# Matrices by turns with the normalisation, filter tables in three buffer sets asked for two steps ahead, and the first set loaded in pieces beside attention

## The chip, the cores and the metric

The kernel runs on one core of a Trainium2 chip. The core has five engines with instruction streams of their own: TensorE (PE in the profile; its weight loads are listed apart as PEld), VectorE (DVE), ScalarE (ACT), GpSimd (POOL) and SyncE (SP, which here only issues DMAs). The metric is the device time of one execution in microseconds.

## The reference

The input is an image tensor of 2 batches, 128 channels and 64 x 64 pixels, so 4096 tokens of 128 channels per batch. Layer 0 normalises over groups of channels and applies rotary attention with four heads, a projection and a residual. Layer 1 does this on the tokens:

```python
t = t + _L1_attn_ref(_ln_t(t))       # softmax(x x^T) x, one head of 128
t = t + _L1_ffn_ref(_ln_t(t), ...)   # STU
```

The second line is a spectral filter. Sixteen filters `phi` (4096 long) are convolved causally with every channel, once as they are and once with alternating signs; the 16 x 2 results of 128 channels are mixed by matrices `M_phi_plus` and `M_phi_minus` scaled by `sigma ** 0.25`, and a short autoregressive term over three taps (`M_u`) is added. Four branches of this kind are weighted by a straight-through choice of `softmax(log_weights + gumbel)`; the branches differ in the length of the sequence that they see, and in their matrices.

## The kernel before

**Layer 0** (`layer0`) goes through four units (batch, pair of heads). In each, two heads times eight blocks of 512 queries are worked through in eleven groups of up to three key tiles: scores on PE (tile `s`), an exponential on ACT (`e`), the weighted sum on PE (`acc`, in PSUM), and at the end of a block a copy to `accs` on DVE (L413). `divide` normalises that with a reciprocal that goes through DRAM by SyncE (`rec`, `back`, `accs<-back`), `project` adds it to the tokens.

Other work is laid beside these groups by Python generators: at certain group numbers `next(beside)` lets one step of it be written into the program. In the last unit the numbers are `BESIDE_LAST`, five of eleven, so 80 slots, and the work is `beside_last`: statistics of batch 0 (nine steps), `normalise` (17; it makes `hi`, `lo`, `bothT`, which are the two halves of the normalised tokens in f16, straight and transposed), `filters16` (12; it makes the filters' spectra and writes them with 32 DMAs and two copies to the DRAM tensor `tables16`) and `matrices16` (33). The last one loads for each of 16 filters the four branches' matrices (`room<-in_mpp`, `room<-in_mpm`, two buffers), takes their weighted sum on DVE (`weighted_sum`, L750 and L752) and writes it to DRAM (`mx`). What is left of the steps is written after the loop.

**Attention of layer 1** (`attend16`) runs for batch 0 and then batch 1 over 36 blocks (j, i) with i not below j. For each block: 24 score matmuls (`y`), exponentials on ACT, a split into two f16 parts (`pair`: a cast on ACT, L1198, a subtraction on DVE, L1199), a transposition of both parts by SyncE's DMA (`eT<-pair`, L1204, only where i is above j), and 12 matmuls of weighted sums with the straight part (`od`) and 12 with the transposed one (`oa`), two blocks later. Beside batch 0 goes the rest of layer 0 (`left`), the statistics of batch 1, `rest16` (masks and means: `mask`, `mu`, `gw`) and the normalisation of batch 1. Beside batch 1 goes `feed(0)`, which transforms the tokens of batch 0, writes them to DRAM (`rows<-uh`) and writes the autoregressive term there too (`base<-oc`), on POOL's queue for batch 0 and SyncE's for batch 1. There are four slots for a block.

**The filters** (the last part, from about 1680 us) run 64 steps (batch, half `ro`, chunk `ch` of eight, stream `s`). A step loads two 1 MB halves of tables and two tiles of tokens (`chunk16`, L1486 and L1491), convolves (16 matmuls `cv`, evacuated by ACT and DVE into two f16 parts `x`) and mixes (48 matmuls `m`). The mixing of one step is written in four parts between the four convolution parts of the next. Tables and tokens have two buffer sets, by turns: the first in a pool of its own (`tables_a`, `early`), the second in the space of `hi` and `lo` (`tables_b`). The loads of a step are written just ahead of its convolution. Beside the first 16 steps goes `feed(1)`, then `back` (L1652 to L1700), which loads `had<-base`, transforms back and adds.

**Order.** A planner with costs of its own orders each engine's instructions and sets the waits; what is written first has priority, and an instruction that is ready can be placed ahead of earlier ones. `tc.keep_in_program_order(ins)` pins an instruction behind the one written just before it on the same engine. The matmuls of `product` and of the filters' steps, and the normalising instructions (`normed`, L743) are pinned. The loads of tables and tokens are not.

Of the kernel before, what the change touches and what calls it, by code (L numbers as in the profile page):

```python
# [32 lines left out]
BESIDE_LAST = (1, 3, 5, 6, 9)  # L33
# [43 lines left out]
def conv_attn_hybrid(ctx: ExitStack, tc: tile.TileContext, io):  # L77
# [39 lines left out]
    def chain(*parts):  # L117
        for p in parts:
            yield from p
# [638 lines left out]
    def layers(st, layer0, in_halves):  # L758
# [52 lines left out]
        def filters16(spare):  # L811
# [21 lines left out]
            yield  # L833
# [115 lines left out]
        def beside_last(stage, spare=None):  # L949
# [4 lines left out]
            yield from normalise(0, stats, lambda i, n: stages[n][:, i])  # L954
            if in_halves:
                yield from filters16(spare)
                yield from matrices16(spare)
# [70 lines left out]
        def means(p, wbr):  # L1028
# [3 lines left out]
            aside.dma_start(gw, io["gw16" if in_halves else "gw"])  # L1032
            if in_halves:
                nc.vector.scalar_tensor_tensor(
                    gw, gw, OUT_SCALE, mask.unsqueeze(1).to_broadcast([P, 2, P]), ALU.mult, ALU.mult
                )
            else:
                nc.vector.tensor_tensor(gw, gw, mask.unsqueeze(1).to_broadcast([P, 2, P]), ALU.mult)

        def rest16(p):  # L1040
            wbr, top = chosen[:2]
            mask_of(p, top)
            yield
            means(p, wbr)
            yield
# [13 lines left out]
        def attend(b, p, beside, closed, ready=lambda i: None):  # L1059
# [111 lines left out]
            for _ in beside:  # L1171
                pass

# [123 lines left out]
        def feed(b, p, bank, fw, stats=None):  # L1297
# [13 lines left out]
            def taps(i, uT):  # L1311
                oc = p.tile([P, 4, P], F32, tag="oc", name=f"oc{b}_{i}", bufs=1)
# [77 lines left out]
        with ExitStack() as l1:  # L1390
# [3 lines left out]
            with ExitStack() as part:  # L1394
# [28 lines left out]
                own = (rest16(p),) if in_halves else (filters(p, fw), matrices(p))  # L1423
                steps = chain(left, stats.steps(), *own, normalise(1, stats, stage, gate))
                (attend16(0, p1, steps, closed) if in_halves else attend(0, p1, steps, closed, ready))
            right0.close()
            if in_halves:
                early = pool(middle, "early", side="right")
                tables_early = [early.tile([P, BP, NS, 2 * NK], F16, name=f"tables_a{n}") for n in range(2)]
                tokens_in = [  # L1430
                    [early.tile([P, NS, C], F16, name=f"tokens{turn}_{n}") for n in range(2)] for turn in range(2)
                ]
            if in_halves:
# [3 lines left out]
            with ExitStack() as part:  # L1437
# [12 lines left out]
                (attend16 if in_halves else attend)(1, p1, feed(0, p, bank, fw), closed)  # L1450
# [7 lines left out]
        if in_halves:  # L1458
            tables_in = [
                tables_early,  # L1460
                [px.tile([P, BP, NS, 2 * NK], F16, tag=f"b{n}", name=f"tables_b{n}") for n in range(2)],
            ]
# [5 lines left out]
        def ordered(instruction):  # L1468
            return tc.keep_in_program_order(instruction)

        def one_bank(name):
            return pc.tile([P, 512], F32, tag="bk", name=name)

# [397 lines left out]
```

## Time and profile before

| | us |
|---|---|
| median of three runs | 2745.54 |
| lowest and highest | 2739.54, 2754.03 |
| the profiled execution | 2742.39 |
| its span, first to last instruction | 2740.6 |
| PE busy | 2579.5 (94%) |
| ACT busy | 1839.1 (67%) |
| DVE busy | 1671.6 (61%) |
| POOL busy | 434.1 (16%) |
| mean granted TensorE clock | 0.98 |

By the trace, layer 0 ends at about 1047 us, the first attention at about 1350, the second at 1680, and the filters take the rest. The profile's matmuls are pipelined and their ends are modelled, so PE's busy time is an upper bound of its work. An arrow in a row means that the left side was waited for, or made, from the right side: `tables_b<-tables` is the load of the tile `tables_b` from the DRAM tensor `tables16`. A wait is put down to what came last. Idle time of an engine that bounds nothing costs nothing. The DMA share is the mean busy share of the 16 DMA engines.

### The profile page before, as it was taken

What the parts mean: (1) busy time and instruction counts of PE and PEld (TensorE: products, weight loads), DVE (VectorE), ACT (ScalarE), POOL (GpSimd) and SP (SyncE); (2) the same over time, 40 slices, a digit from 0 to 9 for tenths busy, and PEclk for the clock granted to TensorE, in tenths of its full rate; (3) what the DMA queues carried; (4) which work ended last, traced back from release to release, by engine and by line L of the source; (5) the groups of instructions that cost most, each with busy time, mean ns of one, the idle gap of its engine ahead of it and who ended that gap; (6) DMA issues with size and microseconds to landing.
All of it is one profiled execution on the core that took longest, in us unless ns stands there. A gap on an engine that the chain in (4) does not pass through costs nothing.

```text
span 2740.6 us, 32562 instructions
## 1 busy us (share of the span) xinstructions
PE 2579.5 (94%) x11955; PEld 1275.5 (47%) x11955; DVE 1671.6 (61%) x2946; ACT 1839.1 (67%) x2059; POOL 434.1 (16%) x711
## 2 busy tenths in 40 slices
PE   5999999999998897899999997999889999999998
PEld 3555555555544453344444443444344445445444
DVE  5256464246358225787887677666556666666664
ACT  4999999999998895566655564444335554555553
POOL 2022021012122301100053101111111111111110
PEclk9999999999999998999999998999999999999999
DMA  5122120012103505676475665666656656656662
GB/s 146 35 66 66 60 74 20 5 53 66 30 29 93 82 7 91 129 123 108 77 151 119 133 108 105 151 177 169 156 156 187 186 192 183 202 195 180 154 197 91
DMA packets 351051, 311.92 MB, mean 114 GB/s; under 512 B 292816, under 2 KB 303200, under 8 KB 334432
## 3 DMA queue, kind: packets, MB, share of 16 engines
q1 hardware_dynamic: 295376, 231.71, 33.3%
q0 software_dynamic: 52512, 74.81, 11.7%
q10 hardware_dynamic: 2992, 3.22, 0.4%
q8 instruction: 96, 1.57, 0.2%
q14 instruction: 75, 0.61, 0.1%
HBM read 212.53 MB, written 23.33 MB: 86 GB/s over the span
## 4 chain that ended last, share of the span: by engine, by line
PE 66%; DMA 14%; DVE 10%; ACT 7%; issue 2%; SPq 0%; POOL 0%; ACTq 0%; DVEq 0%; POOLq 0%
PE m L1565 18%; PE acc L209 12%; PE s L209 11%; PE cv L1549 6%; ACT e L465 5%; PE od L1213 5%; PE y L1185 4%; PE oa L1213 4%; DMA tables_b<-tables 4%; DMA tables_a<-tables 2%; DMA eT<-pair 2%; DMA had<-base 2%; DMA rows<-uh 2%; DVE pair L1199 1%; DVE x L1557 1%
## 5 line engine op out<-in xcount | busy, mean ns | idle before, releaser
L465 ACT ACTIVATE e<-s 128x1536 f16<-128x1536 f32 (+1 forms) x704 | 938.7, 1425 | 54.8 <-PE s L209 50.2
L1557 DVE TENSOR_TENSOR x<-cv,x 128x1024 f16<-128x1024 f32 x512 | 602.7, 1220 | 288.7 <-ACT x L1556 288.5
L1556 ACT CAST x<-cv 128x1024 f16<-128x1024 f32 x512 | 493.8, 1016 | 405.2 <-PE cv L1549 396.0
L1565 PE MATMUL m<-x,mxr 128*128 128x512 f16 x2048 | 625.1, 382 | 0.0
L209 PE MATMUL acc<-e,v 128*97 128x512 f16 x2048 | 559.5, 380 | 16.5 <-DVE accs L413 13.8
L209 PE MATMUL s<-qs,ks 128*128 128x512 f16 x2048 | 560.0, 381 | 7.9 <-ACT e L465 4.3
L1565 PE MATMUL m<-x,mxl 128*128 128x512 f16 x1024 | 393.4, 384 | 2.7 <-DVE oh L1572 2.7
L209 PEld LDWEIGHTS <-v 128*97 128x97 bf16 x2048 | 255.3, 125 | 229.9 <-issue 28.8
L1194 ACT ACTIVATE ey<-y,nshift 128x512 f32<-128x512 f32 x288 | 196.2, 687 | 196.3 <-PE y L1185 151.0
L1565 PEld LDWEIGHTS <-mxr 128*128 128x128 f16 x2048 | 201.8, 99 | 244.6 <-issue 8.2
L209 PEld LDWEIGHTS <-ks 128*128 128x128 f16 x2048 | 201.2, 99 | 230.2 <-issue 47.9
L1486 POOL DMA_DIRECT2D tokens<-rows x252 | 153.4, 613 | 841.9 <-PE cv L1549 815.4
L1185 PE MATMUL y<-bothT 128*128 128x512 f16 x864 | 204.3, 383 | 5.0 <-ACT ey L1194 4.1
L1213 PE MATMUL od<-pair,hi 128*128 128x512 f16 x576 | 185.6, 383 | 19.8 <-DVE pair L1199 14.4
L1199 DVE TENSOR_TENSOR pair<-ey,pair 128x1024 f16<-128x1024 f32 x144 | 175.2, 1219 | 37.8 <-ACT pair L1198 37.6
L1233 DVE SCALAR_TENSOR_TENSOR both<-eT 128x512 f16<-128x512 f16 x224 | 153.7, 686 | 51.6 <-DMA eT<-pair 46.7
L413 DVE COPY accs<-acc 97x512 f32<-97x512 f32 x64 | 44.2, 690 | 228.3 <-PE acc L209 228.2
L1549 PEld LDWEIGHTS <-tokens 128*128 128x128 f16 x1024 | 100.6, 99 | 158.4 <-issue 60.5
L1198 ACT CAST pair<-ey 128x1024 f16<-128x1024 f32 x144 | 150.6, 1046 | 26.6 <-DMA eT<-pair 12.6
L1213 PEld LDWEIGHTS <-hi 128*128 128x128 f16 x1024 | 101.1, 99 | 140.1 <-issue 25.6
L1565 PEld LDWEIGHTS <-mxl 128*128 128x128 f16 x1024 | 101.3, 99 | 132.4 <-DVE oh L1572 9.7
L1213 PE MATMUL oa<-eT,hi 128*128 128x512 f16 x448 | 144.2, 383 | 8.2 <-DMA eT<-pair 8.2
(221 smaller groups left out, 2294.8 us busy)
## 6 DMA issues: line engine op xcount, KB each, us to landing
tables_a<-tables SPq DMA_DIRECT2D x64, 1024.0 KB
tables_b<-tables SPq DMA_DIRECT2D x64, 1024.0 KB
tokens<-rows POOLq DMA_DIRECT2D x252, 128.0 KB, 12.3
tab<-in_rot SPq DMA_DIRECT2D x32, 512.0 KB
ks<-term POOLq DMA_DIRECT2D x112, 64.0 KB, 2.2
qs<-term POOLq DMA_DIRECT2D x112, 64.0 KB, 2.0
accs<-back SPq DMA_DIRECT2D x32, 128.0 KB
room<-in_mpp POOLq DMA_DIRECT2D x16, 256.0 KB, 3.4
```

The costliest lines, as they stand in the source:

```text
L209: tc.keep_in_program_order(nc.tensor.matmul(*args, **kw))
L465: nc.scalar.activation(e[:, own, :], ps[:, own, :], AF.Exp, scale=SCORE_SCALE)
L1185: nc.tensor.matmul(ps[:, q, :], a[0][:, bass.ts(t, P)], c[0][:, bass.ts(i, 512)], start=(n == 0), stop=(n == 2),)
L1194: nc.scalar.activation(e[:, q, :], ps[:, q, :], AF.Exp, bias=nshift16, accum_out=den[:, t, i : i + 1])
L1199: nc.vector.tensor_tensor(pair[:, 1, own], e, pair[:, 0, own], ALU.subtract)
L1213: nc.tensor.matmul(acc, a[0][:, own], pair(m, t), start=(start and t == 0 and n == 0), stop=(stop and t == 3 and n == 2),)
L1233: nc.vector.scalar_tensor_tensor(both, eT[:, 0, :, u, :], 1.0, eT[:, 1, :, u, :], ALU.mult, ALU.add, accum_out=den[:, 4 * i + u, j : j + 1],)
L1486: (nc.gpsimd if n else nc.sync).dma_start(ut[64 * copy : 64 * copy + 64], rows16[b].rearrange("h c r w d -> (h c) r w d")[:, row : row + B ...
L1549: ordered(nc.tensor.matmul(pu[:, h, :], ut[:, at, :], tt[:, :, at, :], start=True, stop=True))
L1556: nc.scalar.copy(hi, pur)
L1557: nc.vector.tensor_tensor(lo, pur, hi, ALU.subtract)
L1565: nc.tensor.matmul(acc, m, x, start=(s == 0 and i == 0), stop=(s == 1 and i == len(products) - 1))
```

## The change

1. `BESIDE_LAST` gets group 0, six slots of eleven.
2. `filters16` is split. Its first part, `branches16` (loads of `phi` and of the transform, branch weights, coefficients), is written at once when the statistics are done. Then one step of the normalisation (and, after it, of the filters) and one step of the matrices are written by turns (`by_turns`).
3. `rest16` issues its three loads (`ends`, `mu_raw`, `gw`) first, on POOL's queue, then the statistics, then the sums that need the loads. `mu_raw` came by ACT's queue before.
4. Tables and tokens have three buffer sets: the early pool, the space of `bothT` (tag `a`), and that of `hi` and `lo` (tags `b0`, `b1`). A step asks for the set of two steps later (`fetch16(steps + 2)`; step 0 asks for 1 and 2). These loads are pinned.
5. The set of step 0 is loaded beside the second attention, after `feed(0)`, each half in four pieces of 256 KB on SyncE, one piece every three slots. Its tokens come by POOL instead of SyncE.
6. `oc` in `feed` has two buffers.

```diff
-BESIDE_LAST = (1, 3, 5, 6, 9)
+BESIDE_LAST = (0, 1, 3, 5, 6, 9)
...
+        def by_turns(*parts):
+            parts = list(parts)
+            while parts:
+                for part in list(parts):
+                    if next(part, parts) is parts:
+                        parts.remove(part)
+                    else:
+                        yield
+
+        def branches16(spare):
...
             chosen.append(coefficients(new, wbr, M_SCALE))
-            yield
+            chosen.append((phi, turned, most))
+
+        def filters16(spare):
+            phi, turned, most = chosen[3]
...
-            yield from normalise(0, stats, lambda i, n: stages[n][:, i])
+            normed = normalise(0, stats, lambda i, n: stages[n][:, i])
             if in_halves:
-                yield from filters16(spare)
-                yield from matrices16(spare)
+                branches16(spare)
+                yield from by_turns(chain(normed, filters16(spare)), matrices16(spare))
...
-        def rest16(p):
+        def rest16(p, steps):
             wbr, top = chosen[:2]
-            mask_of(p, top)
+            ends = p.tile([P, NBR, P], F32, name="ends")
+            aside.dma_start(ends, io["ends"].partition_broadcast(P))
+            mu_raw = p.tile([P, NBR, NU, C], F32, name="mu_raw")
+            aside.dma_start(mu_raw, io["mu"].rearrange("i n d e -> d i n e"))
+            aside.dma_start(gw, io["gw16"])
+            yield from steps
+            weighted_sum(mask, ends, top)
             yield
-            means(p, wbr)
+            weighted_sum(mu, mu_raw, wbr)
...
+        def fetch16(n, pieces=1):
+
+            if n >= len(STEPS):
+                return
+            b, ro, ch, s = STEPS[n]
+            row = FIRST[STREAM[ro, s]]
+            for half in range(2):
+                w0 = 2 * NS * ch + NS * half
+                tt, ut = halves16(n)[half]
+                for copy in range(2):
+                    ordered(
+                        nc.gpsimd.dma_start(
+                            ut[64 * copy : 64 * copy + 64],
+                            rows16[b].rearrange("h c r w d -> (h c) r w d")[:, row : row + BP, w0 : w0 + NS, :],
+                        )
+                    )
+                own = tables16[s, w0 // NS]
+                size = BP // pieces
+                for part in range(pieces):
+                    ordered(
+                        nc.sync.dma_start(
+                            tt[:, part * size : part * size + size],
+                            bass.AP(
+                                tensor=own.tensor,
+                                offset=own.offset + part * size * NS * 2 * NK,
+                                ap=[[NDI * NS * 2 * NK, 8], [NS * 2 * NK, BP], [1, size * NS * 2 * NK]],
+                            ),
+                        )
+                    )
+                    yield
+
+        def spaced(steps):
+            for _ in steps:
+                for _ in range(3):
+                    yield
+
+        def halves16(n):
+            return list(zip(tables_in[n % 3], tokens_in[n % 3]))
...
-                oc = p.tile([P, 4, P], F32, tag="oc", name=f"oc{b}_{i}", bufs=1)
+                oc = p.tile([P, 4, P], F32, tag="oc", name=f"oc{b}_{i}", bufs=2 if in_halves else 1)
...
-                own = (rest16(p),) if in_halves else (filters(p, fw), matrices(p))
-                steps = chain(left, stats.steps(), *own, normalise(1, stats, stage, gate))
+                second = normalise(1, stats, stage, gate)
+                if in_halves:
+                    steps = chain(left, rest16(p, stats.steps()), second)
...
-                    [early.tile([P, NS, C], F16, name=f"tokens{turn}_{n}") for n in range(2)] for turn in range(2)
+                    [early.tile([P, NS, C], F16, name=f"tokens{turn}_{n}") for n in range(2)] for turn in range(3)
...
-                (attend16 if in_halves else attend)(1, p1, feed(0, p, bank, fw), closed)
+                if in_halves:
+                    attend16(1, p1, chain(feed(0, p, bank, fw), spaced(fetch16(0, 4))), closed)
...
-            tables_in = [
-                tables_early,
-                [px.tile([P, BP, NS, 2 * NK], F16, tag=f"b{n}", name=f"tables_b{n}") for n in range(2)],
-            ]
+            second = px.tile([P, 2, BP, NS, 2 * NK], F16, tag="a", name="tables_a")
+            tables_in.append([second[:, n] for n in range(2)])
+            tables_in.append([px.tile([P, BP, NS, 2 * NK], F16, tag=f"b{n}", name=f"tables_b{n}") for n in range(2)])
...
-                            parts = convolve16(u, chunk16(steps, b, ro, ch, s), *xs)
+                            for n in (1, 2) if steps == 0 else (steps + 2,):
+                                for _ in fetch16(n):
+                                    pass
+                            parts = convolve16(u, halves16(steps), *xs)
```

The function `chunk16`, which loaded both halves of a step's tables and tokens just ahead of its convolution, is gone. The tile that was `tables_a` is named `tables_e`; the name `tables_a` is now the set in the space of `bothT`. `mask_of` and `means` remain for the program's other path, which runs only where a range check fails.

## The prediction

> **What bounds the kernel now.** I read the busy time by stage first, then who waits for whom on TensorE in the last part, then the rows in order of time around the two seams. The profiled execution took 2742.4 us (span 2740.6), 3.1 below the median of the three runs, 2745.5. My sum is made against 2742.4; a difference is then taken from the median. From no change a measurement of this kernel can tell about 0.5%, 13.7 us.
>
> Seven stages: length, then busy time of PE, its weight loads, DVE, ACT and POOL, the granted TensorE clock, the DMA share and GB/s.
> ```profile
> core 0: us, PE busy (x) PEld busy (x) DVE busy (x) ACT busy (x) POOL busy (x), PEclk, DMA share, GB/s
> 1047.00:1080.00 33.00, 16.20 (x52) 5.96 (x52) 19.71 (x37) 11.70 (x26) 6.26 (x10) 0.69 0.42 109
> 1100.00:1120.00 20.00, 12.30 (x45) 4.84 (x44) 8.29 (x40) 6.33 (x14) 3.02 (x3) 0.83 0.82 164
> ...
> 1555.00:1680.00 125.00, 124.42 (x584) 57.14 (x582) 98.31 (x223) 79.08 (x164) 5.31 (x4) 1.00 0.59 106
> 1680.00:1704.00 24.00, 9.42 (x29) 3.35 (x30) 15.79 (x43) 8.74 (x9) 4.55 (x6) 0.70 0.56 124
> 1704.00:1960.00 256.00, 242.78 (x1051) 111.56 (x1048) 165.64 (x185) 121.07 (x140) 34.04 (x56) 0.97 0.64 164
> 1960.00:2080.00 120.00, 100.94 (x471) 50.63 (x472) 63.55 (x58) 49.27 (x54) 14.58 (x24) 0.90 0.60 152
> 2080.00:2600.00 520.00, 513.86 (x2460) 244.45 (x2459) 352.74 (x322) 281.04 (x301) 85.49 (x141) 1.00 0.62 186
> ```
> Where PE is 99% busy at clock 1.00 (1555 to 1680, 2080 to 2600) nothing is to be had. In the other five stages PE is idle for 16.8, 7.7, 14.6, 13.2 and 19.1 us, and the lower clock costs up to busy time times (1 - clock): 5.0, 2.1, 2.8, 7.3 and 10.1 us. The pot is 21.8, 9.8, 17.4, 20.5 and 29.2, in all 98.7 us.
>
> PE's waits from 1700 to 2100: total, times, longest.
> ```profile
> PE cv L1549 <- DMA tables_b<-tables: 17.3, 4, 8.9
> PE ar L1320 <- ACT oc L1316: 7.0, 1, 7.0
> PE vt L1667 <- DVE out L1679: 6.5, 1, 6.5
> PE cv L1549 <- DMA tables_a<-tables: 4.2, 4, 2.0
> PE pf L1336 <- DVE uh L1309: 3.7, 1, 3.7
> ```
> Tables cost 21.5 us there: 8.9 at step 1 (1702), 4.7 at about 2005, 7.9 in between.
>
> The seam from layer 0 to the first batch's attention, in order of time; idle time before an instruction stands in brackets:
> ```profile
> 1052.38 0.35 DVE L750 TENSOR_SCALAR room<-room,small 128x256 f32<-128x256 f32 x1 [2.89 <-DMA room<-in_mpm]
> ...
> 1057.82 0.35 DVE L750 TENSOR_SCALAR room<-room,small 128x256 f32<-128x256 f32 x1 [2.54 <-DMA room<-in_mpm]
> ...
> 1061.90 1.01 PE L1213 MATMUL od<-pair,hi 128*128 128x512 f16 x2 [7.24 <-DVE pair L1199]
> ...
> 1069.87 0.29 DVE L750 TENSOR_SCALAR mask<-ends,top 128x128 f32<-128x128 f32 x1 [6.77 <-DMA ends<-in_ends]
> ...
> 1073.35 1.01 PE L1213 MATMUL od<-pair,hi 128*128 128x512 f16 x2 [7.17 <-DVE pair L1199]
> ```
> The attention's subtraction into `pair` stands behind the last matrices on DVE, then behind the mask; both wait for DMAs, and PE twice waits 7.2 us.
>
> SyncE's queue, then TensorE, in order of time:
> ```profile
> 1087.63 1.44 SPq L1491 DMA_DIRECT2D tables_a<-tables  x2
> ...
> 1109.77 0.58 PE L1213 MATMUL oa<-eT,hi 128*128 128x512 f16 x1 [5.31 <-DMA eT<-pair]
> ```
> Step 0's 2 MB of tables were put between the first transposes at 1087; the transposes that follow are late. And the queue's rate:
> ```profile
> 1679.29 1.24 SPq L1491 DMA_DIRECT2D tables_b<-tables  x2
> ...
> 2209.58 7.48 SPq L1491 DMA_DIRECT2D tables_a<-tables  x2
> ```
> An issue into an empty queue takes 0.6 us; in the steady part the second one of a pair is held 6.9 us, so I estimate 6.9 us for 1 MB (152 GB/s), 13.8 for a step's two. A steady step on PE (64 matmuls at 0.216 us) takes 13.8 too: there is no spare rate.
>
> **The change part by part.**
>
> *Matrices by turns, `BESIDE_LAST` with group 0, masks loaded early.* The slots go from 80 to 96 in the last unit; the steps stay about 70, so they end at 70/96 instead of 71/80 of it. The matrices have 9 and 17 fewer steps ahead of them. In the trace twelve of sixteen were done by 898, the last four from 1042 to 1061: the loads of numbers 12 and 13 stood on POOL behind 32 writes of `spectra` (888 to 928). By turns I expect at most two left at the seam, with their data there. `ends`, `mu_raw` and `gw` are issued ahead of the statistics, and DVE's mask stands behind nine steps of these, so the 6.77 us goes. What is late next is the attention's own fill: four exponentials of 0.88, two casts of 1.05 and a subtraction of 1.22, 6.8 us from the first scores, of which PE has two score blocks (5.2 us) to fill. I leave 3 idle and 3 for the clock of the 21.8: **-15**. Bounds: 0 (four matrices still left) to -21.8.
>
> *What that costs in the last unit.* `normed` is pinned behind what was traced before it on DVE, now a matrix's reduction, so the normalisation can wait for loads. Four waits for `room` there take 9.5 us now, and PE loses 13.6 in six waits for `accs` at L413. Bounds: four such waits more, each into PE (+10), to nothing or a gain of 3 where `spectra` no longer meets `accs<-back` (DVE waits 17.1 us for it). DVE is busy 25 of 97 us from 950 to 1047, near nothing: **+3**.
>
> *Step 0's tables leave 1087.* The 9.8 us of that stage go, but DVE (18.6 busy of the 20 us before) is late next: **-7**, bounds 0 and -9.8.
>
> *Eight pieces of 256 KB beside the second batch's attention.* `feed(0)` ends near 1555; a piece every three slots of four a block, some 47 us. By the 6.9 us a piece is 1.7 us on SyncE's queue, among two transposes per block (one pair about 6 us of 7.8). That is 6 + 1.33 x 1.7 = 8.3 of 7.8 us for six blocks, 3 us over, less a diagonal block that transposes nothing. The transposes are wanted over a block later and DVE's waits for them from 1555 on are 2.4 us: **+2**, bounds 0 and, if all eight come into the path, 14. Step 0's tokens move from SP to POOL, which does 5.3 us of work in these 125.
>
> The Trainium skill, DMA: Bandwidth & Descriptors, section Rules for kernel authors, wants 1 MiB or more in a DMA and says that under 64 KB one pays mostly overhead; its fit (2.0 us and bytes by 436 GB/s, on the gpsimd path) gives as an estimate 20.8 us for eight pieces and 8.8 for two whole ones. By that the pieces would cost 12 and the sum below 10 us less; no row of this trace shows a table in pieces.
>
> *Step 1 and 2 at the seam to the filters.* Step 1's set lies in the attention's transposed inputs, free at about 1671, not 1680 as now; so its 13.8 us (22.1 from issue to landing when it met step 2's) end at 1687 to 1694. Step 0's evacuation (eight times 1.22 us on DVE from 1682) ends near 1693, and mixing could begin then, not at 1704: **-10**, bounds -5 and -17.4. Step 2's set is issued at 1680 behind it, done by about 1708, when wanted.
>
> *Two steps ahead, from 1704 on.* A set is now asked for when step n-1's convolution is over and wanted two steps later, about 30 us against a landing of 18 to 28. In the feed stage 7.9 us of table waits and some clock go: **-8**, bounds +3 and -13. The 28.3 us landing near 2005 (4.7 idle, 2.7 clock by ten-microsecond slices): **-6**, bounds 0 and -7.4. What is queued behind the tables on SyncE: `rows<-uh`, `base<-oc`, `had<-base`, which land 14 to 21 us after issue now. `uh` and `had` keep their buffers, so the waits of 3.7 and 6.5 stay; with 4 MB asked for at the start, the first may grow: **+4**, bounds 0 and 10.
>
> *Two buffers for `oc`.* ACT waits 25.5 us in five times for `base<-oc`; PE's 7.0 near 1966 and 2.6 of clock go: **-8**, bounds -4 and -9.6.
>
> `branches16` moves ahead of the normalisation: in the trace its DVE rows already stand there (808 to 813.5). It, the added tiles, the third token set, POOL's token issues (0.6 us each) and the load of `mu_raw` moved from ACT to POOL: nothing, behind a POOL that is busy 34 of 256 us.
>
> Sum: -15 + 3 - 7 + 2 - 10 - 8 - 6 + 4 - 8 = **-45**; 2742.4 becomes 2697, by the median 2745.5 - 45 = **2700**.
>
> **Rivals.**
>
> *The tables' rate is the bound (supply).* For it: 13.8 us of queue against 13.8 us of PE in a steady step, more with `rows` and `base` in the feed stage, and a DMA share of 0.64. Against it: SyncE issues or is held for only 109 of the 170 us from 1752 to 1921, so it has gaps. Then the feed stage, the landing near 2005 and `oc` give nothing, and only the earlier start (8 us) remains: -15 + 3 - 7 + 2 - 8 = -25, 2720.
>
> The same page, section Why a DMA increments its semaphore by 16 and not by 1, says that a transfer runs on as many engines, up to 16, as divide the slowest dimension of both sides. These tables are read with an outer dimension of 8, so by it half of the engines carry them, and buffers don't widen that. The share of 0.62 at 99% PE agrees. By the rule the sum is this rival's 2720, by the gaps in the rows 2700.
>
> *The seam stays.* The planner leaves four matrices, or the mask, ahead of `pair`, and turns cost the last unit 10: -45 + 15 + 7 = -23, 2722. For it: twelve matrices ran ahead without turns already. Against it: 36 us from 1000 to 1036 in which DVE has little to do.
>
> *All of it comes back.* Every term at its good end except the waits for `had` and `uh`: about -73, 2672.
>
> *Slower: turns chain the last unit to the loads.* In turn, a matrix's buffer is free again only after its store (2.0 us to landing), two issues (1.5) and a load (3.7), 7.2 us. If `normed` and then L413 stand behind that each time and PE behind L413, sixteen times cost 115 us; against 48 gained elsewhere that is 2812. It decides from (48 + 14) / 7.2, nine turns on. For it: the pin on `normed`. Against it: two buffers halve it, DVE has other work, and PE lost only 13.6 us with twelve matrices in the same stretch.
>
> **How the numbers follow.** Forecast 0.51 (2682 to 2718), supply 0.17, seam 0.14, all of it 0.09, slower 0.09. The range 2672 to 2745 leaves out the slower case and the tails, under 0.2. Faster by over 0.5% (below 2732): the forecast, all of it, and two thirds of the two rivals at 2720, 0.80; within: the other third, 0.11; slower 0.09.
>
> **What would show it.** Right: no `room` or `ends` wait on DVE after 1047 and PE's 7.2 us waits gone; no tables before the second attention, and no 5.3 us wait for `eT` near 1109; the first `m` at about 1693 less the earlier gains; no table waits of PE after it; no wait for `oc`. Wrong: table waits as long as now with SyncE held more of the time (supply); `accs` waits over 30 us from 790 to 950 (turns); `eT` waits in the second attention's late half; longer waits for `uh` or `had`.

## The result, and the profile after

The changed kernel takes 2742.9 us (median of 12 runs, 2728.6 to 2752.7) against 2740.7 for the kernel before measured beside it; the ratio is 1.0004, with a 95% interval of 0.9982 to 1.0026. So nothing is gained, where the prediction said 2700. A ratio leaves out a few executions in which the chip was in a slower state; a median counts them all. The profiled execution took 2752.7 us (span 2750.9), the slowest of the twelve and some 10 us above their median; e13 below has a profile of the same kernel at 2722.2 us.

First the same stages as before (length, busy time of PE, its weight loads, DVE, ACT and POOL, granted TensorE clock, DMA share, GB/s):

```profile
1047.00:1080.00 33.00, 30.76 (x147) 14.66 (x146) 26.45 (x58) 24.54 (x51) 2.13 (x2) 1.00 0.52 101
1100.00:1120.00 20.00, 20.00 (x94) 9.07 (x93) 18.44 (x42) 12.75 (x26) 0.00 (x0) 1.00 0.57 107
...
1680.00:1704.00 24.00, 17.88 (x81) 8.16 (x79) 11.85 (x15) 7.18 (x8) 2.43 (x4) 0.98 0.61 140
1704.00:1960.00 256.00, 218.71 (x933) 100.80 (x934) 149.61 (x167) 111.67 (x129) 30.39 (x50) 0.93 0.64 147
1960.00:2080.00 120.00, 104.83 (x493) 52.11 (x492) 64.36 (x59) 49.66 (x55) 14.58 (x24) 0.91 0.59 167
2080.00:2600.00 520.00, 502.85 (x2393) 238.15 (x2392) 342.48 (x313) 272.71 (x292) 83.89 (x138) 0.99 0.61 185
```

The two early seams are closed: PE is busy 30.8 of 33 us where it was 16.2, and 20.0 of 20 where it was 12.3, both at clock 1.00. The filters also begin earlier: the first mixing matmul `m` starts at 1671.4 instead of 1704. Up to there the change is 32 us ahead, and the terms of the prediction up to that point (-15, +3, -7, +2, -10) make 27. From there to the end the kernel before needs 2740.6 - 1704 = 1037 us of its span, the changed one 2750.9 - 1671.4 = 1079. The gain goes in the stage where `feed(1)` runs beside the filters: in 1704 to 1960 PE is busy 218.7 of 256 us at clock 0.93, and it was 242.8 at 0.97.

What PE waits for between 1700 and 2100 (total, times, longest):

```profile
PE pf L1403 <- DVE uh L1376: 28.7, 3, 15.6
PE vt L1709 <- DVE out L1721: 11.3, 2, 9.2
PE uT L1422 <- DVE uh L1376: 9.0, 1, 9.0
...
PE pf L1403 <- DMA rows<-uh: 2.8, 1, 2.8
PE cv L1591 <- DMA tables_a<-tables: 1.5, 1, 1.5
...
PE cv L1591 <- DMA tables_e<-tables: 0.5, 1, 0.5
```

The 7.0 us for `oc` are gone, and in this window the waits for tables fall from 21.5 us to 2.0. They do not all go: from 2080 to 2600, where the kernel before waits for none, this execution waits 8.0 us for tables (4.7 + 2.3 + 1.0), and the one of e13 waits 11.0 us (6.2 + 3.1 + 1.7) in the first window and none in the second. So about half of these waits go. In their place stand 40.5 us for `uh` (28.7 + 9.0 + 2.8; 3.7 before, 28.9 in e13). DVE is not slow there. It waits for ACT's half of `uh`, and ACT's waits from 1660 to 2200 say what for:

```profile
ACT uh L1375 <- DMA rows<-uh: 60.9, 5, 19.6
```

A buffer of `uh` comes free when its four writes to `rows` have landed. These stand on SyncE with the tables. SyncE's issues, with the time that each took (the second number; x2 are two issues and what lies between them):

```profile
1648.23 1.22 SPq L1222 DMA_DIRECT2D tables_a<-tables  x2
1655.98 1.19 SPq L1222 DMA_DIRECT2D tables_b<-tables  x2
1665.22 4.84 SPq L1222 DMA_DIRECT2D tables_e<-tables  x2
...
1683.21 10.48 SPq L1410 DMA_DIRECT2D rows<-uh  x1
...
1733.85 1.27 SPq L1222 DMA_DIRECT2D tables_b<-tables  x2
...
1735.73 1.26 SPq L1222 DMA_DIRECT2D tables_e<-tables  x2
...
1760.17 10.48 SPq L1409 DMA_DIRECT2D rows<-uh  x1
```

Three sets, 6 MB, are asked for within 22 us; later two whole sets stand together (1733.85 and 1735.73); and the issue of a single write of 64 KB is held for 10 us (12.5 at most). In the chain that ended last, from 1640 to 2150, writes of `rows` now make 28%, `had` 10% and tables 11%; before, `rows` made 8%, `had` 7% and tables 31%. Some of its pieces (start, length in us):

```profile
1683.21 28.75 DMA rows<-uh
1741.92 36.84 DMA rows<-uh
1779.51 22.51 DMA tables_a<-tables
...
1850.16 33.08 DMA rows<-uh
...
1899.28 22.64 DMA rows<-uh
...
1985.31 29.47 DMA had<-base
```

### The profile page after: what moved, and what is told of

The parts are those of the page before. It is cut to its first block, busy times and chain, and to the rows that moved or that the text cites. A ratio compares the mean times of both kernels' runs of the same rounds, so it can differ in the third digit from the quotient of the medians.

```text
span 2750.9 us, 32560 instructions
## 1 busy us (share of the span) xinstructions
PE 2580.7 (94%) x11955; PEld 1276.4 (46%) x11955; DVE 1671.5 (61%) x2946; ACT 1838.6 (67%) x2059; POOL 437.6 (16%) x716
## 3 DMA queue, kind: packets, MB, share of 16 engines
q1 hardware_dynamic: 295920, 231.18, 33.4%
q0 software_dynamic: 53296, 76.13, 12.2%
## 4 chain that ended last, share of the span: by engine, by line
PE 63%; DMA 18%; DVE 10%; ACT 6%; issue 2%; SPq 0%; POOL 0%; DVEq 0%; ACTq 0%; POOLq 0%
PE m L1607 17%; PE acc L209 11%; PE s L209 11%; PE cv L1591 5%; DMA rows<-uh 5%; PE od L1280 5%; ACT e L465 5%; PE y L1252 5%; PE oa L1280 4%; DMA had<-base 4%; DMA eT<-pair 2%; DMA tables_b<-tables 2%; DMA tables_a<-tables 2%; DVE x L1599 1%; DVE pair L1266 1%
## 6 DMA issues: line engine op xcount, KB each, us to landing
tokens<-rows POOLq DMA_DIRECT2D x256, 128.0 KB, 14.3
```

## The experiments

The theory from these rows (queue): the change gains about what was predicted, and the writes of `rows` and `base`, which share SyncE's queue with two or three table sets, give it back through the buffers of `uh`. The rivals: the tables' rate is the bound and any other place is as good (supply); the buffers alone are too few; the gain at the early seams was never real. Ratios are to the kernel before on the same chip, with 95% intervals; a difference of some 10 us (0.4%) is the least that two of them can tell. Where two ratios are divided here their relative half-widths are added as squares.

### The writes on another queue (e1, e14), and the changed kernel beside it (e13)

```diff
-            queue = aside if b == 0 else nc.sync
+            queue = aside if b == 0 or in_halves else nc.sync
```

> The changed kernel with one edit: the second batch's feed writes `rows` and `base` by POOL's queue, not SyncE's. Theory 'queue': in the changed kernel these writes land 22 to 37 us after issue, behind two table sets on SyncE's queue, and the two `uh` buffers stop ACT (60.9 us in five waits) and through it PE (40.5 us for `uh`). Then these waits go, with some clock: 2690 to 2705 us. Theory 'supply': the tables' rate is the bound and the waits only show it. Then PE waits for tables instead, and the time stays within 10 us of 2743.

> The changed kernel itself, beside the two runs below on one chip, so that what the writes' queue is worth is read in one place. Both theories: no different from the kernel before within 0.5%, 2732 to 2758 where that is 2745. It is the base for the next two.

> Once more the writes of rows and base on POOL, beside the changed kernel. Queue theory: 30 to 48 us below the changed kernel, as the waits for uh (40.5 with the clock's part behind them) go and come back with 7 to 14; the ratio to the kernel before 0.982 to 0.989. If the first run's 0.986 was partly that chip, as the later 0.992 with had on POOL makes possible, it is 15 to 28 below, ratio 0.990 to 0.994, and then the queue explains half of what was missing.

Measured: e1 2700.6 us, ratio 0.9857 (0.9821 to 0.9892). On another chip, beside each other: the changed kernel (e13) 2744.7, 0.9971 (0.9930 to 1.0012), and the writes on POOL (e14) 2707.2, 0.9837 (0.9782 to 0.9893). Moving the writes off SyncE is worth 37 us there, and 42 if e1 is set against the 2742.9 of the changed kernel's first runs. That e1 lands at the predicted 2700 is chance: it is another kernel than the one that was predicted, and e15 below is quicker still. PE's waits from 1640 to the end, in e1:

```profile
PE vt L1709 <- DVE out L1721: 16.5, 3, 8.9
PE pf L1403 <- DVE uh L1376: 6.9, 1, 6.9
PE uT L1422 <- DVE uh L1376: 6.5, 1, 6.5
```

The waits for `uh` fall from 40.5 (28.9 in e13) to 13.4, and there is none for tables. The writes on SyncE's queue are what costs, and the supply rival falls: the same tables come in time, while the DMA engines move more (177 GB/s from 1704 to 1960 in e1, 147 in the changed kernel, 150 in e13).

### The same move in the kernel before (e5)

The edit of e1 made in the kernel before; nothing of the change.

> The kernel before with one edit: the second batch's feed writes `rows` and `base` by POOL's queue. Two buffer sets, one step ahead, the old seam. Theory 'queue' (the writes stand behind tables on SyncE, and two sets ahead doubled that): before, `uh` cost PE 3.7 us, `oc` 7.0 and part of the 21.5 of table waits came from tables held behind writes, so 2722 to 2735 us; the rest of the 41 us that POOL's queue gave the changed kernel belongs to the change. Rival 'writes only' (the change adds nothing once the writes are off SyncE's queue): 2700 to 2712 us.

Measured: 2736.2 us, ratio 1.0012 (0.9970 to 1.0053), above both expectations. Its waits for tables and `oc` stay, and 14.3 us more are put under "issue", time in which PE waited for nothing that the profile shows (3.0 before):

```profile
PE cv L1549 <- DMA tables_b<-tables: 13.0, 3, 9.6
PE ar L1320 <- ACT oc L1316: 7.6, 2, 7.3
```

So this move alone gains nothing, and the change alone gains nothing; together they gain 1.4 to 1.6%.

### More buffers instead of another queue (e2)

```diff
-                        uh = p.tile([P, 2, 4, C], F16, tag="uh", name=f"uh{b}_{i}_{c}")
+                        uh = p.tile([P, 2, 4, C], F16, tag="uh", name=f"uh{b}_{i}_{c}", bufs=4 if b else 2)
```

> The changed kernel with one edit: four `uh` buffers in the second batch's feed instead of two. The writes stay on SyncE's queue and land as late as now. 'Queue': nobody needs them early, so the waits for `uh` go all the same, 2695 to 2712 us (a little less than with POOL's queue, since `had` and `base` stay behind the tables in both). 'Supply': 2733 to 2750 us, with waits for tables in their place.

Measured: 2731.7 us, 0.9956 (0.9925 to 0.9987); 2731.7 lies between the two expectations. The waits for `uh` are gone, and tables are waited for somewhat longer: 17.8 us from 1640 on, 10.0 and 11.0 in the changed kernel's two profiles. The profiled execution took 2708.8 us, near the quickest of this kernel, so it does not show where the median's 23 us more go:

```profile
PE cv L1591 <- DMA tables_a<-tables: 7.6, 2, 4.4
PE cv L1591 <- DMA tables_b<-tables: 6.3, 2, 3.3
PE cv L1591 <- DMA tables_e<-tables: 3.9, 1, 3.9
```

SyncE takes one issue after the other. With the writes still there and still held (up to 12.9 us), what is late now is the tables behind them. Buffers move a part of the wait; only 11 us go with them, about a quarter of what e1 gains.

### One step ahead instead of two (e3, e10)

```diff
-                            for n in (1, 2) if steps == 0 else (steps + 2,):
+                            for n in (steps + 1,):
```

e3 makes this edit in the changed kernel, e10 in e1.

> The changed kernel with one edit: a step asks for the set of the next step, not of two later, three buffer sets as they are. At most about one set stands ahead of a write on SyncE's queue. 'Queue': the writes land after 15 to 22 us, about as before the change, most of the 40 us of `uh` waits go, table waits of 10 us or so come back: 2705 to 2725 us. 'Supply': as the changed kernel or slower, 2740 to 2760 us.

> The writes on POOL, tables fetched one step ahead instead of two, three buffer sets kept. With the writes on SyncE, one step ahead was faster (2721 against 2743), which by the queue theory is since fewer sets stand before a write. With the writes elsewhere nothing is left for one step ahead to gain, and the term for two steps ahead (8, bounds -3 and 13) is lost: 2702 to 2714, table waits of TensorE from 1700 on over 15 us. If two steps ahead is itself a loss (more tables in flight slow all DMAs), it is faster than 2700: 2685 to 2697.

Measured: e3 2721.2 us, 0.9944 (0.9906 to 0.9981); e10 2735.2, 0.9988 (0.9951 to 1.0025). The same edit has both signs. With the writes on SyncE it makes the kernel quicker, by 0.6% with a half-width of 0.4%. That agrees with fewer sets ahead of a write: PE has no wait for `uh` left. But it waits 59.5 us for tables, where 10 were expected (in a profiled execution of 2756.2 us, the slowest of the twelve). With the writes on POOL the edit loses 1.3% (0.9988 / 0.9857), some 36 us, more than the 2 to 14 that was expected. In e10 PE waits again (and 17.6 us more for tables; for the 26.3 under "issue" the profile shows no cause):

```profile
PE cv L1591 <- issue: 26.3, 5, 12.9
PE cv L1591 <- DMA tokens<-rows: 17.1, 5, 9.2
```

So two steps ahead is worth having, and was hidden by the queue that it filled.

### The rows' writes alone (e15)

```diff
-                            queue.dma_start(to[:, c, h, 2 * i : 2 * i + 2, :], uhr[:, h, :, 0, :])
-                            queue.dma_start(to[:, c, h, at : at + 2, :], uhr[:, h, :, 1, :])
+                            (aside if in_halves else queue).dma_start(to[:, c, h, 2 * i : 2 * i + 2, :], uhr[:, h, :, 0, :])
+                            (aside if in_halves else queue).dma_start(to[:, c, h, at : at + 2, :], uhr[:, h, :, 1, :])
```

> Only the writes of rows (uh) move to POOL; base stays on SyncE behind the tables. The trace after has its long waits in uh (37.7 us of TensorE's) and 17.4 in the sums with had, which read base. If uh alone is the cause, this gives what all the writes on POOL give, within 8 us. If base counts too, the waits for had (vt behind out) stay over 15 and oc waits come back, and this stands 10 to 20 us above all the writes on POOL.

Measured: 2685.1 us (2668.4 to 2699.4), ratio 0.9768 (0.9710 to 0.9826): 60 us below the changed kernel on the same chip (56 by the ratios, with a half-width of 20), and 22 below e14. Both branches of the expectation missed on the good side. PE is full, at clock 1.00, where the changed kernel had 218.7 at 0.93 and 104.8 at 0.91, and in e13 226.2 and 104.9, both at 0.94 (the profiled execution of e15 is its quickest, as e13's is, so these two are the ones to compare):

```profile
1704.00:1960.00 256.00, 253.34 (x1139) 119.78 (x1140) 177.33 (x191) 132.34 (x152) 79.84 (x120) 1.00 0.63 195
1960.00:2080.00 120.00, 119.80 (x591) 59.05 (x589) 82.53 (x73) 64.58 (x70) 19.40 (x32) 1.00 0.60 168
```

In the waits of the queue itself, the writes of `base` stay on SyncE and wait there for their data; the issues of the tables, held up to 13.0 us in the changed kernel, are not held any more. First the waits, 1640 to 2150:

```profile
SPq L1222 <- PE cv L1591: 284.0, 47, 11.0
SPq L1391 <- DVE oc L1390: 111.2, 8, 20.8
```

and then the groups of issues on the tables' line, 1640 to 1960 (ns: least, median, most):

```profile
L1222 SPq DMA_DIRECT2D tables_a<-tables x14: 574/575/597, 1651.8 to 1941.0; - x14
...
L1222 SPq DMA_DIRECT2D tables_e<-tables x12: 574/575/607, 1668.9 to 1927.2; - x12
```

The same view of the changed kernel:

```profile
L1222 SPq DMA_DIRECT2D tables_a<-tables x11: 574/591/9574, 1648.2 to 1951.7; - x11
...
L1222 SPq DMA_DIRECT2D tables_e<-tables x10: 574/594/13027, 1665.2 to 1940.0; - x10
```

The holds come with the writes of `rows` on this queue: they are gone in e14 and e15, where these are elsewhere, and stay in e2 and e3, where they are not. (e7 below shows that the writes alone do not make them.)

### Load on POOL, or pacing (e16)

```diff
-                queue.dma_start(base[b][:, 4 * i : 4 * i + 4, :], oc)
+                (nc.scalar if in_halves and b else queue).dma_start(base[b][:, 4 * i : 4 * i + 4, :], oc)
```

made in e15.

> Writes of rows on POOL, those of base on ScalarE's queue, so that SyncE issues tables and had alone. Two accounts of why base on SyncE (2685) beats base on POOL (2707). Load on POOL's queue: 256 KB of base stand ahead of rows and tokens there; with base on ScalarE they don't, and this is as fast as 2685 or within 8 us of it. Pacing: base on SyncE holds that queue for 111 us in eight waits for oc, so that fewer table sets share the engines with rows and tokens; without that hold this is like all writes on POOL, 2700 to 2712, with waits for uh of 10 to 16 us back on TensorE.

Measured: 2701.7 us, 0.9863 (0.9817 to 0.9909), like the writes all on POOL (0.9837), and 17 us from e15 on another chip (26 by the ratios, with a half-width of 20). So it isn't the load of `base` on POOL's queue. PE waits 8.6 us for `uh`, a little less than the pacing account said. Where it shows is the tokens' landing time (1640 to 1960: least, median, most). In e14:

```profile
DMA to landing us min/median/max: 3.8/17.2/30.3
```

in e15:

```profile
DMA to landing us min/median/max: 3.9/13.3/27.9
```

and in e16:

```profile
DMA to landing us min/median/max: 5.1/16.9/31.0
```

With `base` on SyncE the tables are asked for later (SyncE is held 111 us by eight waits for `oc`), and tokens land 4 us sooner. With `base` on POOL or ACT SyncE asks for a set as soon as a buffer is free (it waits 399 us for `cv` in e14, 284 in e15), long before the set is wanted, and the tokens share the engines with it. This agrees with pacing; that a pace set on purpose, without `base`, would do the same was not tried.

### The rows' move in the kernel before (e17)

The edit of e15 made in the kernel before.

> The kernel before, with its writes of rows on POOL and nothing else. If the rows' place in the queue were the whole matter, the kernel before would gain the most of the 60 us too: 2690 to 2710. If the change's parts are what gains and the rows only stood in the way, it keeps its seams, its late step 1 and its table waits: 2730 to 2745, as all its writes on POOL gave (2736).

Measured: 2712.1 us, 0.9916 (0.9882 to 0.9951), between the two. The kernel before lost 23 us (half-width 9) to the same queue: its 7.0 us for `oc` go without a second buffer, and its 6.5 for the sums with `had` too. What is left is what the change is for:

```profile
PE cv L1549 <- DMA tables_b<-tables: 13.6, 3, 9.5
PE cv L1549 <- DMA tables_a<-tables: 4.0, 2, 2.2
```

Over this kernel the change is worth 0.9768 / 0.9916 = 0.9851, with half-width 0.0068: 41 us (22 to 59) by the ratios, 27 by the two medians. Between e5 and e17 lies only the place of `base`: 24 us, on two chips, as between e14 and e15 on one (22). So in e5 moving `base` took away what moving `rows` gives.

### The seam from layer 0 (e4, e6, e9, e18)

e4 makes the kernel before with the last unit, group 0 and the masks of the change; the other three take these out of the changed kernel (e6), of e1 (e9) and of e15 (e18):

```diff
-BESIDE_LAST = (0, 1, 3, 5, 6, 9)
+BESIDE_LAST = (1, 3, 5, 6, 9)
...
-                branches16(spare)
-                yield from by_turns(chain(normed, filters16(spare)), matrices16(spare))
+                yield from normed
+                branches16(spare)
+                yield
+                yield from filters16(spare)
+                yield from matrices16(spare)
...
         def rest16(p, steps):
+            yield from steps
             wbr, top = chosen[:2]
-            ends = p.tile([P, NBR, P], F32, name="ends")
-            aside.dma_start(ends, io["ends"].partition_broadcast(P))
...
-            yield from steps
-            weighted_sum(mask, ends, top)
+            mask_of(p, top)
```

> The kernel before with only the changes to the last unit and to the loads of masks and means; tables and tokens as before. PE's idle time at the seam from layer 0 falls by the 15 us term, while step 0's tables still go between the first transposes. 'Queue' (the seam's gain is real and was given back in the filters): 2722 to 2732 us. Rival 'seam lost': what the seam gains is given back by the last unit or by a later start of something else, 2736 to 2748 us.

> The changed kernel with the old last unit (normalisation, then filters, then matrices; five slots of eleven) and the old order of masks and means. If the seam's gain is its own, this is 12 to 18 us above the changed kernel, 2752 to 2762, with PE's two waits of about 7 us for `pair` back at 1060. If the seam doesn't matter, 2738 to 2748.

> The writes of rows and base on POOL (2700.6 when run), with the last unit's matrices again behind the filters, the old group list and the masks loaded late. The run with the seam alone (2737) left open whether its gain is real. If the seam's gain is kept as soon as the feed stage is free, this is slower by the term of the prediction, 12 (15 less 3), to the whole pot of 21.8: 2712 to 2722, with the 7.2 us waits for pair back twice. If the gain at the seam is always given back later, for instance because DMAs set the pace from layer 0 to the end, it is 2698 to 2706.

> Writes of rows on POOL (2685), with the last unit, the group list and the masks of before. With TensorE at 253 of 256 us in the feed stage nothing is left there that could give a seam's gain back, so the term shows at its price: 12 to 22 us above 2685, 2697 to 2707, with two waits of 7.2 us for pair. If the seam is given back wherever DMAs bind later, it is within 6 us: 2682 to 2691.

Measured: e4 2737.4 us, 0.9979 (0.9943 to 1.0016); e6 2748.9, 1.0051 (1.0013 to 1.0089); e9 2722.0, 0.9932 (0.9894 to 0.9969); e18 2703.6, 0.9879 (0.9830 to 0.9927). e4 by itself decides nothing. The other three are slower than the kernels that they were made from by 0.5% (13 us; 6 by the two medians), 0.75% (21) and 1.1% (31, with half-width 0.75%; 18 by the two medians). PE's waits of e18 from 787 to 1640 bring the seam back:

```profile
PE od L1280 <- DVE pair L1266: 14.0, 2, 7.4
```

All three agree with the term of the prediction, 15 less 3, within wide intervals.

### The had loads on POOL too (e11), and four buffers for uh with it (e12)

```diff
-                    nc.sync.dma_start(had, baser[:, ro, 4 * p4 : 4 * p4 + 4, :])
+                    nc.gpsimd.dma_start(had, baser[:, ro, 4 * p4 : 4 * p4 + 4, :])
```

made in e1; e12 adds the edit of e2.

> The writes on POOL, and the load of had (the halves read back from base) issued on POOL too, so that only tables are left on SyncE in this part. Queue theory: had stood behind a table set, as the writes did; of the 16.5 us in which TensorE waits for the sums with had (vt behind out), some 6 to 12 go: 2688 to 2696. If had is late because its buffer is free late (one set of them) or because the base writes land late, nothing changes: 2698 to 2704.

> As the run before, and four buffers for uh in the second batch. TensorE still waits 13.4 us for uh with the writes on POOL. If these are waits for buffers that a write of 64 KB holds while it shares the engines with 2 MB of tables, they go: 8 to 13 us less than the run before, 2678 to 2688. If the time goes into table waits instead, as when four buffers were given with the writes on SyncE (17.8 us of them), it is the run before's within 5 us.

Measured: e11 2724.8 us, 0.9921 (0.9884 to 0.9957); e12 2731.1, 0.9922 (0.9880 to 0.9964): both worse than e1 and e14. e11 met neither branch of its expectation; e12 is the same as e11, as its second branch said, but not through waits for tables: it has none. PE's waits of e11 from 1640 on:

```profile
PE vt L1709 <- DVE out L1721: 30.7, 3, 14.0
PE cv L1591 <- DMA tokens<-rows: 7.8, 3, 3.2
```

The load of `had` has one buffer, and the tokens of the next steps are queued behind it on POOL, which waits for that buffer (`had` for the sum that reads it, 1900 to 2600):

```profile
POOL had L1703 <- DVE out L1721: 111.6, 9, 24.0
```

The order of the queue is again what costs: an instruction that waits was put in front of loads that were free to go. e12's waits for `uh` are gone and its 31.3 us for `vt` remain, so nothing is gained by them.

### Twice the DMA engines (e7, e8)

The prediction weighed a rule of the Trainium skill (DMA: Bandwidth & Descriptors, section Why a DMA increments its semaphore by 16 and not by 1), by which an outer dimension of 8 puts a transfer on half of the engines. In e7 each half of a set comes as eight transfers of 16 partitions; e8 adds the edit of e1.

```diff
-                for part in range(pieces):
+                for g in range(8):
                     ordered(
                         nc.sync.dma_start(
-                            tt[:, part * size : part * size + size],
+                            tt[BP * g : BP * g + BP],
                             bass.AP(
                                 tensor=own.tensor,
-                                offset=own.offset + part * size * NS * 2 * NK,
-                                ap=[[NDI * NS * 2 * NK, 8], [NS * 2 * NK, BP], [1, size * NS * 2 * NK]],
+                                offset=own.offset + g * NDI * NS * 2 * NK,
+                                ap=[[NS * 2 * NK, BP], [1, BP * NS * 2 * NK]],
```

> The changed kernel with each 1 MB half loaded by eight transfers of 16 partitions in place of one whose outer dimension is 8 (step 0's too, in place of the four pieces). Same bytes, same buffers. If the outer dimension of 8 keeps a load on half of the DMA engines, 1 MB takes 3.5 to 4.5 us and not 6.9, the writes behind it land in about half of the time, and the `uh` waits shrink: 2700 to 2720 us. If not, the loads take as long and SyncE issues 16 transfers a step at 0.58 us: 2743 to 2765 us.

> The same eight transfers of 16 partitions with the feed's writes on POOL's queue. If the loads are faster so, this is the fastest: 2690 to 2700 us, with `had` landing in 10 us and not 20. If the loads are not faster: 2700 to 2720 us.

Measured: e7 2779.6 us, 1.0143 (1.0074 to 1.0213); e8 2818.9, 1.0293 (1.0230 to 1.0356). The stages of e7:

```profile
1704.00:1960.00 256.00, 226.57 (x956) 102.64 (x955) 151.03 (x168) 112.26 (x130) 31.50 (x52) 0.95 1.02 156
2080.00:2600.00 520.00, 474.84 (x2233) 223.67 (x2231) 319.25 (x292) 252.88 (x271) 76.37 (x126) 0.97 1.02 169
```

The DMA share goes from 0.61 to 1.02 in the steady part, which agrees with the rule; but the bytes per second fall from 185 to 169. A part of e7's expectation came true: on SyncE, and still in small packets (26,625 of 32,350 under 512 B from 1704 to 1960), the writes land in 5.7 us in the median, and none of their issues takes over 1.1 us (12.5 in the changed kernel).

```profile
rows<-uh SPq DMA_DIRECT2D x64, 64.0 KB, 5.7
```

Yet PE still waits 23.5 us for `uh`, and now the tables are the pace. In the steady part SyncE waits 282 us for earlier transfers of tables, where it waited 362 us for `cv`, that is for PE, in the changed kernel; and tables make 42% of the chain that ended last, 9% there. So more engines did not bring the tables sooner. What bounds the smaller transfers, and why e8 is 39 us slower than e7, isn't shown by any row here.

## Why the prediction was wrong

By its own steps:

*The seam (-15), the last unit (+3), the tables out of 1087 (-7).* Right. The waits for `pair` fall from 14.4 us to 0.8, those for `eT` from 8.2 to 0.9, and both windows are full. The turns cost nothing that shows: PE waits 13.5 us for `accs` in the last unit, 13.6 before. e9 and e18 price the seam at 18 to 31, e6 at 6 to 13.

*Eight pieces beside the second attention (+2).* Right in size: they are issued from 1519.6 to 1561, and from 1500 to 1570 PE is busy 65.4 of 70 us at clock 0.98, where it was 66.3 at 1.00 before. That is some 2 us, and not the 12 that the fit of the Trainium skill (DMA: Bandwidth & Descriptors, section Anatomy of one DMA — SWDGE (gpsimd) path) gave as an estimate in the prediction.

*Step 1 and 2 at the seam to the filters (-10).* Right: the first `m` is 32 us earlier, of which the terms before it explain 17.

*Two steps ahead (-8), the long landing (-6), two buffers for `oc` (-8).* The waits that they were priced from went in part: tables from 21.5 to 10 or 11 from 1640 on (none in e1 and e15), `oc` from 7.0 to 0. But part of that was one cost counted under several names. e17 shows that 23 us of the kernel before, `oc` and `had` among them, were the writes of `rows` on SyncE, and would go by moving these alone.

*What is queued behind the tables on SyncE (+4, bounds 0 and 10).* This is the step that failed. The prediction named the place ("with 4 MB asked for at the start, the first may grow") and mis-sized it. On one chip the changed kernel loses 60 us to this queue (e13 less e15: 2744.7 - 2685.1), the kernel before 23 to 28 (e17), so the change added 32 to 37, with a half-width of some 20, where the term had 4 and the bound 10. With 34 in place of 4 the sum is -15. The change measured within 0.3% of none, so some 15 us of the forecast gain remain unaccounted for, 10 at the near end of the interval; the double count above can be a part of it, which no run here singles out. With the writes of `rows` on POOL in both kernels the change is worth 27 to 41 us of the 45 (e15 against e17).

Its size could have been had from two things that were at hand. In the kernel before `feed(1)` makes 16 `uh` between 1712 and 1927, one in 14 us, in two buffers, so a write may take some 28 us (two times 14) before PE feels it. And by the prediction's own rows a set took 22.1 and 28.3 us to land where two sets met, and the writes took 14 to 21 us behind what then stood there. With three buffer sets two whole ones stand together ahead of writes again and again, and then the 28 are used up at once: the chain has pieces for `rows` of 22 to 37.

*The price of 6.9 us for 1 MB itself* was misread. In the steady part of the kernel before the row of two issues has 7.48 us, but each issue takes 0.574 us (least, median and nearly the most), and SyncE waits there for `cv`, that is for PE to free a half. The issues on the tables' line and then SyncE's waits, 2080 to 2600, both of the kernel before:

```profile
L1491 SPq DMA_DIRECT2D tables_b<-tables x36: 574/574/643, 2084.5 to 2587.6; - x36
```

```profile
SPq L1491 <- PE cv L1549: 413.8, 67, 10.3
```

So the 13.8 us of queue that matched PE's 13.8 us a step were PE's own pace, no rate of the tables; the number that spoke for the supply rival was not about the tables at all. In the feed stage of the same trace issues of tables do take up to 8.2 us. That difference, between a stage with the writes of `rows` and one without, was the sign to read.

*The rivals.* Supply is refuted by e1 and e15 (no wait for tables, at 177 and 195 GB/s from 1704 to 1960 where the changed kernel had 147). "The seam stays" and "turns chain the last unit" are refuted by the rows after. "All of it comes back" (2672) is near what e15 does, 2685 and in its quickest run 2668, but only with the writes of `rows` moved, which the change did not do.

## What to carry to other kernels

Before deeper prefetching, list every other instruction on the queue that issues it, and hold how long a write there may take before its buffer is wanted against the bytes that can now stand ahead of it. A change and a cure that each gain nothing alone (the change, e5) can gain together (e14): undo the new wait on top of the change, not in place of it. And move one thing at a time: e5 gained nothing because it moved `base` too (e17). And a pair of issues that takes long is a rate only if the issuing engine's own waits say so: look whether it waited for a consumer.

## What was not expected of the hardware

The writes of `rows` take another form on the other queue. The packets of all queues, 1700 to 1960, in the changed kernel:

```profile
DMA packets 27751, 38.16 MB, mean 147 GB/s; under 512 B 22169, under 2 KB 22169, under 8 KB 24611
```

and in e15:

```profile
DMA packets 18331, 50.70 MB, mean 195 GB/s; under 512 B 9367, under 2 KB 9879, under 8 KB 14019
```

Over the whole span the hardware queue of SyncE has 17,408 packets fewer in e15 (295,920 against 278,512) and POOL's 2,048 more (55,344 against 53,296), for the same 64 writes of 64 KB: 272 packets each on SyncE, 32 on POOL. So the move changed both the order of the queue and the size of the packets, and no run here parts the two cleanly. e7 bears on it: there the writes are on SyncE in small packets and hardly held, so small packets alone do not hold an issue; they were held only with loads of 1 MB on the same queue. The Trainium skill (DMA: Bandwidth & Descriptors, section Specifications) gives 512 B as the least for full rate, and the packets of these writes on SyncE are below it (64 KB in 272 packets is 241 B each).

The same page, section Issuing engines are not separate DMA queues, says that starting DMAs on several engines only saves the sequencer's time to initiate them, which is usually small relative to the DMA. Here that time was not small: the issue of a write of 64 KB took 0.42 us in the median but 12.5 at most in the changed kernel and 15.4 in e13, and 0.71 to 0.75 on POOL, and with the buffers behind it the choice of the engine, with the form of the packets that goes with it, is worth 60 us of 2745.

A queue that waits can help: `base` on SyncE, which holds the tables back 111 us, makes the kernel 17 to 22 us faster than `base` on ACT or POOL (e15 against e16 and e14).

The version with the writes of `rows` alone on POOL (e15) beats both kernels: 2685.1 us, ratio 0.9768 (0.9710 to 0.9826).
